# Depthwise convolutions as column-tiled products over shifted copies, state sums in fours, and a different placing of third stages in a four-layer kernel on one core

## The chip, the cores and the metric

The kernel runs on one core of one Trainium2 chip. A core has four compute engines with queues of their own: TensorE (PE; its weight loads are listed as PEld), VectorE (DVE), ScalarE (ACT) and GpSimd (POOL). SyncE (SP) computes nothing; here it issues nearly all DMAs, which sixteen DMA engines carry out. The metric is device time in microseconds for one execution of the whole program; lower is better.

## The reference, cut to what matters

The input `x` is 4 images of 96 channels, 64 x 64 pixels, float32. Four layers follow each other, each on the group-normalised `x` and added to it:

```python
x = x + _L0_conv_ref(_gn(x), ...)
x = x + _L1_conv_ref(_gn(x), ...)
x = x + _L2_conv_ref(_gn(x), ...)
x = x + _L3_conv_ref(_gn(x), ...)
```

Layer 0 is attention with queries pooled 2 x 2 (3 heads of 32 channels, 1,024 queries, 4,096 keys), a softmax over nine neighbours, and a depthwise 5 x 5 convolution of the values:

```python
lepe = lax.conv_general_dilated(v, lepe_w, (1, 1), [(2, 2), (2, 2)], feature_group_count=C)
...
out = feature + lepe
out = jnp.einsum('oc,bchw->bohw', proj_w, out) + proj_b[None, :, None, None]
```

Layer 1 is a selective scan of 192 channels with 16 states each, in four directions over the 4,096 pixels, between convolutions:

```python
xi, z = jnp.split(jnp.einsum('bchw,oc->bohw', x, in_proj_w), 2, axis=1)
xi = jax.nn.silu(conv2d(xi, conv_w, conv_b, groups=E, pad=1))
xs = jnp.stack([xf, xf[..., ::-1], xt, xt[..., ::-1]], axis=1)
...
y = jnp.einsum('bkdln,bknl->bkdl', h, c) + Ds[None, :, :, None]
...
t = jax.nn.relu(bn(conv2d(u, c1_w, c1_b), ...))
t = jax.nn.relu(bn(conv2d(t, c2_w, c2_b, groups=2 * E, pad=1), ...))
t = conv2d(t, c3_w, c3_b)
s = t.mean((2, 3))
...
return t + t * s[:, :, None, None]
```

`c1` takes 192 to 384 channels with a 1 x 1 kernel, `c2` is a depthwise 3 x 3 of 384 channels, `c3` takes them to 96. Layer 2 is one 3 x 3 convolution (sharpening). Layer 3 begins with two 1 x 1 products, goes through two depthwise 3 x 3 convolutions of the same 96 channels, one to a gated branch (`dw2`, `ag1`, `ag2`) and one to a second selective scan with a depthwise 3 x 3 of its own, and ends with a layer norm and the block `crm`. So four places hold depthwise convolutions: `lepe` (5 x 5, 96 channels), the one in front of each scan (3 x 3, 192 channels), `c2` (3 x 3, 384) and `dw1`, `dw2` (3 x 3, 96 each).

## The kernel before, in words

**The scan units.** The function `streams` runs eight scans in the order of `SCANS`: layer 1 of images 0 and 1, layer 3 of images 0 and 1, then the same for images 2 and 3. A scan is four directions x four chunks of 1,024 pixels x two halves of 96 channels, that is 32 groups; a group is twelve units, a unit 8 channels x 16 states on 128 partitions over 1,024 pixels. That makes 384 units a scan and 3,072 in all. One call of `unit(i)` issues, in this order:

- `fetch(i + 4)` (L1938 to L1940): a DMA of 512 KB on SP that copies 8 channels' step sizes from DRAM to all 128 partitions of a tile `rep` (10 buffers);
- DMA issues that were postponed with `later(n, f)` and have become due (`catch_up`), and the store of a finished `yo`;
- `decays(i + 2)` (L1948): exp in place on `rep`, ScalarE;
- `scan(i)` (L1969): the recurrence along the pixels, VectorE, into `hs`; `carry_on` copies its last column, ScalarE;
- `times_c(i)` (L1981): `hs` times C, GpSimd, back into `rep`;
- `collect(j)`, in every third unit, four units late: the sums over 16 states on TensorE. Three units' products stand beside each other in three groups of 32 columns and write three blocks of 32 partitions of the accumulator `acc`;
- `drive(i + 2)`: two small products that spread step size times input over the states, TensorE, into `bx` in PSUM;
- `times_b(i + 1)` (L1962): `bx` times B, VectorE;
- at the end of a group `output`: `acc` goes to `yo` and with it to DRAM (`y_row`, `y_col`, 96 rows).

`prepare` makes what a group of units needs (step sizes, their bf16 parts, B and C) a group or two ahead. In the region of the units the order of instructions on every engine is the order of this program (`tc.manual_schedule`); nothing reorders it.

**The other work beside the units.** All other layers are written as generators that yield after short steps: `first(b)` (layer 0, then the projection and the convolution in front of the first scan), `second(b)` (what follows the first scan up to what the second needs: layer norm, `c1`, `c2`, `c3`, squeeze, sharpening, `dw1`, `dw2`), `third(b)` (what follows the second scan) and `last(b)`. A generator yields nothing when it has issued a product whose result another engine then takes, a number of slots when it has done so, or a tuple when it has just issued one of a chain of products. `BESIDE` says what runs beside which scan; a scan's budget grows by `PACE` slots in each unit (3.5 beside a `first`, 3.7 beside a `second`, 3.2 beside the thirds), less 2.1 in the units that collect. What has not been used up 19 units before the end of a scan is issued there at once (`work.run()`). `first(0)` runs before all units, the rest of `last(3)` after them.

```python
BESIDE = ((("first", 1),), (("second", 0),), (("second", 1),), (("first", 2),),
          (("first", 3),), (("second", 2),), (("second", 3),), (("third", 0), ("third", 1), ("third", 2), ("last", 3)))
```

**Depthwise convolutions before.** The image stands in a tile with a border (`vpad`, `upad`, `hp`, or the two `band` tiles that hold ten rows each). `diagonals` (L1112) makes, on GpSimd, a table of diagonal 96 x 96 matrices, one a tap. `conv` issues one product a tap over a shifted window of the tile, all into one bank of PSUM: 25 for `lepe`, 9 elsewhere, each one slot. Every product goes through the helper `mm` (L948), so all of TensorE's work has that line; it is told apart by the names of its tiles. Before the units begin (`solo`), VectorE takes 11 of the 25 taps or 4 of the 9. `second` has 384 channels as four groups of 96, so 32 convolutions of 9 products an image, then `dw2` with its gates, then `dw1`, then `in_conv` (projection of all rows, then the convolution of all).

Of the kernel before, what the change touches and what calls it, by code (L numbers as in the profile page):

```python
# [26 lines left out]
BIG = LEPE + L  # L27
CH = 1024
# [10 lines left out]
          (("first", 3),), (("second", 2),), (("second", 3),), (("third", 0), ("third", 1), ("third", 2), ("last", 3)))  # L39
# [13 lines left out]
def _weights(i):  # L53
# [13 lines left out]

    p = {}
# [9 lines left out]
    def scan(tag, in_w, conv_w, conv_b, xp, dtw, dtb, alog, d):  # L78
        p[tag + "in"] = in_w.T
        p[tag + "conv"] = halves(conv_w.reshape(E, 9))  # L80
        p[tag + "conv_b"] = halves(conv_b)

# [34 lines left out]
    for n in ("dw1_w", "dw2_w"):  # L117
        p["l3_" + n] = a[n].reshape(C, 9)
    p["l3_ag1"] = a["ag1_w"].reshape(C // 2, C).T
# [24 lines left out]
def _constants(i):  # L144
# [28 lines left out]

    for tag, w in (("l1_", i["L1_conv_A_log"]), ("l3_", i["L3_conv_ss_Alog"])):
        c[tag + "alogn"] = w.reshape(4, E // 8, 8, N).transpose(3, 2, 0, 1).reshape(128, 4, E // 8)
# [4 lines left out]
    c["spread"] = s.reshape(128, 128)  # L180
    return c
# [712 lines left out]
def streams(ctx: ExitStack, tc: tile.TileContext, x, wts, cst, out, wat, cat, flag):  # L894
# [13 lines left out]
    n0, n1, n2 = (cat[k][0] for k in ("ones", "addn", "l1_alogn"))  # L908
# [40 lines left out]

    solo = [True]  # L950
# [37 lines left out]
    def batch_norm(tag, bias):  # L988
        s, b = derived(4), derived(4)
        inv_std(s, wv(tag + "v"))  # L990
        nc.vector.tensor_mul(s, s, wv(tag + "g"))
        nc.vector.tensor_sub(b, bias, wv(tag + "m"))
        nc.vector.tensor_mul(b, b, s)
        nc.vector.tensor_add(b, b, wv(tag + "b"))
        return s, b

    bn1 = batch_norm("l1_bn1_", wv("l1_c1_b"))
    bn2 = batch_norm("l1_bn2_", wv("l1_c2_b"))
# [8 lines left out]
    with tc.tile_pool(name="start", bufs=1) as T:  # L1007
        t0 = T.tile([128, cst.shape[1] - n2], F32, name="t0")
        nc.scalar.dma_start(out=t0, in_=cst[:, n2:])
# [7 lines left out]
        for tag in ("l1_", "l3_"):  # L1017
# [7 lines left out]
            dsum[tag] = derived(2)  # L1025
            nc.vector.tensor_reduce(dsum[tag], wv(tag + "d"), AX.X, ALU.add)


    def image(name):
        return [dram.tile([96, L], F32, name=f"{name}{b}") for b in range(B)]  # L1030

    res1, res2, gate1, skip3, gate3 = (image(k) for k in ("res1_", "res2_", "gate1_", "skip3_", "gate3_"))
    u_row, u_col, y_row, y_col = ([image(f"{k}{h}_") for h in range(2)] for k in ("urow", "ucol", "yrow", "ycol"))
# [73 lines left out]
    def diagonals(pool, w, name="diag"):  # L1107

        taps = w.shape[1]
        w = w[:, :taps]  # L1110
        d = pool.tile([96, taps, 96], F32, tag=name, name=name, bufs=1)
        nc.gpsimd.tensor_tensor(  # L1112
            d,
            ident[:96, :96].unsqueeze(1).to_broadcast([96, taps, 96]),
# [238 lines left out]
    def first(b):  # L1353

        with tc.tile_pool(name="p1", bufs=1) as P:
# [4 lines left out]
            with tc.tile_pool(name="p1d", bufs=1) as D:  # L1360
                samp = D.tile([96, 34, 34], F32, name="samp")
                dist = D.tile([96, 34, 34], F32, name="dist")
                for t in (samp, dist):
                    border(t, 1)
# [836 lines left out]
```

## Time and profile before

Three runs of the kernel before took 14,713.78 to 14,727.14 us, median 14,725.35 us. The profile is of one execution, whose span is 14,698.9 us.

| quantity | value |
|---|---|
| span of the profiled execution | 14,698.9 us |
| median of three runs | 14,725.35 us |
| `scan` with carry, L1969, VectorE | 2,304 x 2,344 ns |
| `times_c`, L1981, GpSimd | 3,072 x 2,357 ns |
| `times_b`, L1962, VectorE | 3,072 x 1,212 ns |
| `decays`, L1948, ScalarE | 3,072 x 1,143 ns |
| `drive`, products into `bx`, TensorE | 6,144 records, 1,412.7 us |
| state sums, products into `acc`, TensorE | 12,288 records, 2,586.7 us |
| depthwise products, `band`, `upad`, `hp`, `vpad` | 2,304, 2,016, 1,152, 1,200 records; 3,291.1 us |
| `rep` fetches | 3,072 x 512 KB |

A group of instructions in the profile has its line, engine, operation, tiles written and read with their shapes, the number of instructions, their busy time, the mean of one in ns, and the idle time of the engine just before them with what ended most of it. A float32 product leaves two records for each call of `mm`. The clock shown for TensorE is what the chip granted it, as a share of full speed; a stretch of the run is given by its start and end in us, and its row has the length, the busy time of PE, PEld, DVE, ACT and POOL with the number of instructions, the granted clock, the DMA engines' busy share and GB/s.

### The profile page before, as it was taken

Reading aid. Unit: us, or ns where it says so; the run is one execution under the profiler, and the core shown is the slowest. Engines: PE = TensorE matmul, PEld = TensorE weight load, DVE = VectorE, ACT = ScalarE, POOL = GpSimd, SP = SyncE. Lnnn points to the kernel's source line nnn. Section 1 sums busy time; section 2 is a strip of 40 time slices with the busy share of each in tenths; the row PEclk is TensorE's granted clock in tenths of the full one; section 3 lists DMA queues with packets and bytes.
Section 4 is the critical chain, followed back from the end, with each engine's and each line's share of the span. In section 5 each row is a group of like instructions: output and inputs, shape, how many; then the busy total and the mean of one; then the engine's idle time right before and its main releaser. Section 6 shows DMA issues by size and latency. Waiting matters only on the chain.

```text
span 14698.9 us, 128101 instructions
## 1 busy us (share of the span) xinstructions
PE 12296.5 (84%) x40802; PEld 3348.5 (23%) x40802; DVE 11654.4 (79%) x7509; ACT 8721.7 (59%) x12340; POOL 10204.0 (69%) x4634
## 2 busy tenths in 40 slices
PE   8888987988889796889868887897979888777767
PEld 2322221222223121222212222222212222111111
DVE  0477888888878888778887888788888888778776
ACT  3355565556756666554755556566755567666554
POOL 0166787777868778667776788687777777666564
PEclk9878887988879787778867887897979888677666
DMA  0266787787878778667876778687787878776674
GB/s 9 72 158 163 188 212 198 188 204 184 221 175 200 197 199 209 154 166 193 211 189 160 178 200 220 172 205 189 203 200 189 204 190 215 175 181 169 165 182 108
DMA packets 902735, 2644.27 MB, mean 180 GB/s; under 512 B 107104, under 2 KB 257216, under 8 KB 902048
## 3 DMA queue, kind: packets, MB, share of 16 engines
q1 hardware_dynamic: 901392, 2634.72, 71.8%
q8 instruction: 324, 5.31, 0.2%
q14 instruction: 363, 2.97, 0.1%
q10 hardware_dynamic: 656, 1.27, 0.0%
HBM read 2168.97 MB, written 466.62 MB: 179 GB/s over the span
## 4 chain that ended last, share of the span: by engine, by line
PE 50%; DVE 20%; ACT 10%; DMA 7%; issue 6%; POOL 5%; SPq 1%; DVEq 0%; POOLq 0%; ACTq 0%
PE one L948 33%; DVE hs L1969 14%; PE acc L948 9%; PE bx L948 6%; DVE bx L1962 5%; DMA rep<-dd 3%; PE held L948 3%; POOL rep L1981 2%; ACT rep L1948 2%; ACT L1948 1%; ACT ex L1287 1%; ACT L1890 1%; DMA xz<-gate 0%; ACT delta L1888 0%; POOL delta L1893 0%
## 5 line engine op out<-in xcount | busy, mean ns | idle before, releaser
L1981 POOL TENSOR_TENSOR rep<-hs,bc 128x1024 f32<-128x1024 f32 x3072 | 7224.5, 2357 | 3210.5 <-DVE hs L1969 2664.2
L1969 DVE TENSOR_TENSOR_SCAN hs<-rep,carry,bx 128x1024 f32<-128x1024 f32 x2304 | 5401.7, 2344 | 274.0 <-POOL rep L1981 14.8
L1962 DVE TENSOR_TENSOR bx<-bx,bc 128x1024 f32<-128x1024 f32 x3072 | 3723.6, 1212 | 1086.2 <-PE bx L948 1063.5
L1948 ACT ACTIVATE rep<-rep,l_decay 128x1024 f32<-128x1024 f32 x3072 | 3495.7, 1143 | 513.3 <-DMA rep<-dd 493.8
L948 PE MATMUL bx<-parts,spread 24*128 24x512 bf16 x6144 | 1412.7, 435 | 1662.7 <-DVE hs L1969 1608.8
L948 PE MATMUL acc<-rep,ct 128*32 128x512 f32 x12288 | 2586.7, 741 | 9.8 <-POOL rep L1981 9.1
L1969 DVE TENSOR_TENSOR_SCAN hs<-rep,bx 128x1024 f32<-128x1024 f32 x768 | 1754.7, 2285 | 123.3 <-ACT carry L1977 29.0
L948 PEld LDWEIGHTS <-spread 24*128 24x128 bf16 x6144 | 310.4, 93 | 4154.6 <-DVE hs L1969 2755.2
L948 PE MATMUL one<-band,dg 96*96 96x512 f32 x2304 | 1075.9, 605 | 0.0
L948 PE MATMUL one<-upad,diag 96*96 96x512 f32 x2016 | 996.4, 632 | 0.0
L948 PE MATMUL one<-qq,kk 96*128 96x512 f32 x1152 | 818.8, 800 | 134.6 <-ACT ex L1287 84.0
L948 PEld LDWEIGHTS acc<-rep,ct 128*32 128x32 f32 x12288 | 506.2, 127 | 1742.4 <-issue 1494.2
L1287 ACT ACTIVATE ex<-one 128x512 f32<-128x512 f32 x576 | 343.1, 596 | 747.7 <-PE one L948 743.0
L948 PE MATMUL one<-pr,ct 6*96 6x512 f32 x1024 | 652.7, 728 | 84.3 <-DVE V L1192 10.4
L1948 ACT ACT_TABLE_LOAD x495 | 635.1, 1283 | 76.6 <-DMA rep<-dd 68.5
L948 PE MATMUL one<-hp,diag 96*96 96x512 f32 x1152 | 607.1, 668 | 28.6 <-POOL diag L1112 28.6
L948 PE MATMUL one<-vpad,diag 96*96 96x512 f32 x1200 | 611.7, 647 | 0.0
L1977 ACT COPY carry<-hs 128x1 f32<-128x1 f32 x2304 | 409.2, 178 | 308.4 <-DVE hs L1969 306.5
L948 PE MATMUL held<-ex,cols 128*32 128x256 f32 x3072 | 567.9, 450 | 7.9 <-ACT ex L1287 1.9
L948 PE MATMUL held<-ex,vT 128*32 128x256 f32 x3072 | 568.3, 451 | 0.0
L948 PEld LDWEIGHTS one<-band,dg 96*96 96x96 f32 x2304 | 346.6, 162 | 535.3 <-issue 516.8
L948 PEld LDWEIGHTS one<-upad,diag 96*96 96x96 f32 x2016 | 314.7, 169 | 489.2 <-issue 478.3
(3420 smaller groups left out, 14369.3 us busy)
## 6 DMA issues: line engine op xcount, KB each, us to landing
rep<-dd SPq DMA_DIRECT2D x3072, 512.0 KB
parts<-du SPq DMA_DIRECT2D x1024, 144.0 KB
bc<-rows SPq DMA_DIRECT2D x256, 512.0 KB
dd<-delta SPq DMA_DIRECT2D x256, 384.0 KB
du<-cut SPq DMA_DIRECT2D x256, 384.0 KB
us<-urow SPq DMA_DIRECT2D x128, 384.0 KB
du<-cut SPq DMA_DIRECT2D x256, 192.0 KB
yrow<-yo SPq DMA_DIRECT2D x128, 384.0 KB
```

The source lines that it names most:

```text
L948: nc.tensor.matmul(o, lhsT=lhsT, rhs=rhs, start=first, stop=last)
L1287: nc.scalar.activation(last.rearrange("p a b -> p (a b)"), p, AF.Exp, scale=HD**-0.5)
L1890: nc.scalar.activation(w, w, AF.Ln)
L1948: nc.scalar.activation(a, a, AF.Exp, scale=decay[tag][:, k, NG * h + m : NG * h + m + 1])
L1962: nc.vector.tensor_mul(bx, bx, ready[i // NG][2][:, 0, :])
L1969: nc.vector.tensor_tensor_scan(out=hs, data0=a, data1=bx, initial=carry[:, h, m : m + 1] if c else 0.0, op0=ALU.mult, op1=ALU.add)
L1977: nc.scalar.copy(carry[:, h, m : m + 1], live[i][1][:, CH - 1 : CH])
L1981: nc.gpsimd.tensor_tensor(a, hs, ready[i // NG][2][:, 1, :], ALU.mult)
```

## The change

**Tables.** `diagonals` and `conv` go, and with them VectorE's share of the taps. `blocks` makes, on GpSimd, tables of 32 columns: for each group of 32 channels and each step in y, three (for `lepe` four) 32 x 32 diagonals stacked on the partitions, one for each shift.

**Shifted copies.** A bordered image has a row pitch of 65 (`ROW`; the column of zeros is shared by neighbouring rows), 66 for `lepe`. Before a convolution, `copies` brings it from SBUF to SBUF by DMAs of 32 partitions each into a tile `around` (2 buffers): three copies of a group of 32 channels, shifted by 0, 1 and 2 columns, stand on 96 partitions. So one product with a table of 96 x 32 covers three taps of 32 channels, and the 3 or 4 groups of 32 channels stand beside each other in 32-column tiles (`shifted`). For `lepe` four copies (0 or 1 row, 0 or 1 column) stand on 128 partitions, and nine products with steps of 2 cover a 6 x 6 kernel whose last row and column are zero.

```diff
+    def soon(f):
+
+        done = []
+        if solo[0]:
+            f()
+            return [True]
+        later(1, lambda: done.append(f()))
+        return done
+
+    def arrived(done):
+        while not done:
+            yield WAIT
+
+    def copies(T, S, at, n, of=range(3)):
+
+        for s in range(3):
+            for g, m in enumerate(of):
+                nc.sync.dma_start(out=T[32 * s : 32 * s + 32, g, :n], in_=S[32 * m : 32 * m + 32, at + s : at + s + n])
+
+    def shifted(o, weight, T, groups, row):
+
+        for y in range(3):
+            for g in range(groups):
+                rhs = T[:, g, (row + y) * ROW : (row + y + 8) * ROW].rearrange("p (r c) -> p r c", c=ROW)[:, :, 0:W]
+                mm(o[32 * g : 32 * g + 32], weight[:, g, y, :], rhs, y == 0, y == 2)
+            if y < 2:
+                yield (1,)
+        yield
```

Copies are issued through `soon`: beside the units they go out one unit later on SP, and the generator yields `WAIT` until then. A `fill` has 9 copies of 18 rows (in front of the scans, `dw1` and `dw2`: two blocks of 8 rows), 12 copies of 10 rows (`c2`: one block) or 12 of 12 rows (`lepe`). Each convolution is run one fill later than its fill.

**What follows from the new shapes.** `c1`'s 384 channels stand as 3 groups of 128 partitions, not 4 of 96, so `c1`, `c2`, the batch norms and `c3` have three steps for four. `dw2` and `dw1` use the same copies and run in one loop, the gates' products after both; `x1` moves to an outer pool. `in_conv` projects and convolves in turn instead of one after the other. The keys `kk` of the attention stand in the tile `feat`. `lepe`'s loads of `x` come with the fills, and the projection of the values alternates with the convolution.

```diff
-                    for q in range(4):
-                        p = bank()
-                        yield from conv(p[:96], dg[q], last[:, q], 0)
-                        nc.scalar.activation(t2[:, q, :], p[:96], AF.Relu,
-                                             bias=bn2[1][:, q : q + 1], scale=bn2[0][:, q : q + 1])
-                        yield 1
...
+                def fill(k):
+                    j, q = divmod(k, 3)
+                    T = pool.tile([96, 4, 10 * ROW], F32, name="around", bufs=2)
+                    src = band[j % 2][:, q, :]
+                    there[k] = T, soon(lambda: copies(T, src, 0, 10 * ROW - 1, range(4)))
+
+                def convolve(k):
+                    j, q = divmod(k, 3)
+                    T, done = there.pop(k)
+                    yield from arrived(done)
+                    if q == 0:
+                        t2[j] = pool.tile([128, 3, PCH], F32, name="t2", bufs=1)
+                    p = bank()
+                    yield from shifted(p, dg[:, 4 * q : 4 * q + 4], T, 4, 0)
+                    nc.scalar.activation(t2[j][:, q, :], p, AF.Relu, bias=bn2[1][:, q : q + 1], scale=bn2[0][:, q : q + 1])
+                    yield 1
```

**State sums in fours.** `collect` runs in every fourth unit, five units late, with four groups of 32 columns; 24 of each 32 rows of `acc` hold sums. `rep` has 12 buffers, `yo` is one tile of 128 rows for the whole run, `y_row` and `y_col` have 128 rows, and what reads them takes 24 of each 32 rows with four DMAs (`ungapped`) where there was one.

```diff
-        rep = sp.tile([128, CH], F32, name="rep", bufs=10)
+        rep = sp.tile([128, CH], F32, name="rep", bufs=12)
...
-        hs = [live.pop(i + q)[0] for q in range(3)]
-        w = addn[:, 24 - 8 * (m // 3) : 56 - 8 * (m // 3)]
+        hs = [live.pop(i + q)[0] for q in range(4)]
+        w = addn[:, 24 - 8 * (m // 4) : 56 - 8 * (m // 4)]
         for e in range(2):
-            for q in range(3):
-                mm(live["acc"][bass.ts(q, 32), bass.ts(e, PCH)], w, hs[q][:, bass.ts(e, PCH)], m == 0, m == NG - 3)
+            for q in range(4):
+                mm(live["acc"][bass.ts(q, 32), bass.ts(e, PCH)], w, hs[q][:, bass.ts(e, PCH)], m == 0, m == NG - 4)
...
-        j = i - BEHIND - 2
-        due = j >= 0 and j % 3 == 0
+        j = i - BEHIND - 3
+        due = j >= 0 and j % 4 == 0
```

**Order and pace.** The third stages of images 0 and 1 move from the last scan to the sixth and seventh, behind the second stages of images 2 and 3. The pace is given for each scan.

```diff
-          (("first", 3),), (("second", 2),), (("second", 3),), (("third", 0), ("third", 1), ("third", 2), ("last", 3)))
+          (("first", 3),), (("second", 2), ("third", 0)), (("second", 3), ("third", 1)), (("third", 2), ("last", 3)))
+PACE = (2.25, 2.05, 2.05, 2.25, 2.25, 2.75, 2.75, 3.2)
...
-            owed = min(owed, 0.5) + PACE[BESIDE[s][0][0]] - (2.1 if i % 3 == 1 else 0.0)
+            owed = min(owed, 0.5) + PACE[s] - (2.1 if i % 4 == 1 else 0.0)
```

The program is also built with a setting of 1,024 for its dynamic DMA scratch.

## The prediction

> **What bounds the kernel now.** I read the shares and slices of the page first, then busy time by stretches, then the products of two tiles at one clock, then the waits.
>
> ```profile
> PE 12296.5 (84%) x40802; PEld 3348.5 (23%) x40802; DVE 11654.4 (79%) x7509; ACT 8721.7 (59%) x12340; POOL 10204.0 (69%) x4634
> ...
> PEclk9878887988879787778867887897979888677666
> ...
> q1 hardware_dynamic: 901392, 2634.72, 71.8%
> ```
>
> TensorE is busiest, but at 0.6 to 0.9 of its clock; VectorE is close behind; the one DMA queue moved 2,634.72 MB in 71.8% of 14,698.9 us, 10,554 us or 4.01 us per MB.
>
> The next view splits the run: busy time (and instructions) of each engine, granted clock, DMA share, GB/s.
>
> ```profile
> 0.00:690.00 690.00, 607.35 (x2724) 217.84 (x2724) 180.45 (x284) 211.56 (x352) 32.12 (x43) 0.95 0.10 28
> 690.00:14569.00 13879.00, 11600.58 (x37948) 3108.96 (x37948) 11444.46 (x7184) 8486.50 (x11948) 10167.06 (x4588) 0.81 0.76 189
> 14569.00:14699.00 130.00, 88.61 (x134) 21.68 (x130) 29.48 (x42) 23.68 (x42) 4.82 (x3) 0.63 0.12 34
> ```
>
> From 690 to 14,569 the 3,072 scan units run, 13,879 us, with VectorE (third busy number) at work for 11,444. Its work there does not change, so only its 2,435 us of idle time can shrink. These two groups show why 3,072 × (2.34 + 1.21) = 10,906 of it stays:
>
> ```profile
> L1969 DVE TENSOR_TENSOR_SCAN hs<-rep,carry,bx 128x1024 f32<-128x1024 f32 x2304 | 5401.7, 2344 | 274.0 <-POOL rep L1981 14.8
> L1962 DVE TENSOR_TENSOR bx<-bx,bc 128x1024 f32<-128x1024 f32 x3072 | 3723.6, 1212 | 1086.2 <-PE bx L948 1063.5
> ```
>
> The second names the idle time: 1,063.5 us waiting for the product `bx` of `drive`, which stands in TensorE's queue behind work of the other layers. Where, by kind of that work, one image each (the columns as above):
>
> ```profile
> 804.00:1621.00 817.00, 717.66 (x3305) 197.03 (x3304) 623.10 (x381) 470.94 (x719) 561.63 (x251) 0.79 0.66 163
> 1621.00:2300.00 679.00, 607.22 (x1864) 169.50 (x1864) 600.22 (x363) 434.25 (x599) 551.65 (x245) 0.88 0.82 211
> 2394.00:2665.00 271.00, 221.34 (x566) 53.54 (x567) 201.36 (x147) 141.23 (x208) 164.26 (x78) 0.77 0.67 166
> 2665.00:3049.00 384.00, 382.63 (x1230) 116.14 (x1229) 337.93 (x195) 234.91 (x341) 312.88 (x137) 0.99 0.80 197
> 3152.00:3589.00 437.00, 346.76 (x1008) 91.15 (x1009) 347.14 (x219) 277.45 (x392) 317.94 (x147) 0.79 0.74 184
> 3589.00:3880.00 291.00, 277.24 (x864) 79.88 (x862) 253.14 (x148) 222.59 (x275) 238.63 (x108) 0.94 0.84 215
> 3880.00:3970.00 90.00, 69.91 (x235) 18.45 (x234) 85.49 (x51) 68.14 (x91) 77.22 (x34) 0.85 0.93 245
> 3970.00:4064.00 94.00, 47.92 (x160) 8.37 (x160) 84.61 (x50) 47.83 (x52) 77.13 (x35) 0.57 0.86 207
> 12531.00:13533.00 1002.00, 784.51 (x2009) 176.17 (x2010) 787.21 (x557) 622.02 (x878) 632.39 (x293) 0.72 0.70 173
> ```
>
> VectorE's idle time is length less busy time. Attention and neighbours (first row): 194 us, three images, 582. Convolutions of `first` (second row) 79, three images, 236; of `second` (rows four, six and seven) 46 + 38 + 5 = 89, four images, 354; together 590. Hand-offs of `second` (rows three and five: layer norm, sharpening, gates): 70 + 90 = 160, four images, 638. Thirds of images 0 and 1 (last row): 215. That leaves 410 in the remaining parts. The reader should see that the convolutions, where TensorE is fullest (382.63 of 384), lose little: 12%, beside 10% in the row with no beside-work (3970). The loss per microsecond is largest where products are handed between engines at a clock of 0.7 to 0.8.
>
> **The change, part by part.** Products first. One view each of the same full-clock stretch, by tile: the depthwise product of `band`, then the state sums `acc`.
>
> ```profile
> 2762.00:3049.00 287.00, 158.51 (x341) 51.30 (x342) 18.30 (x28) 0.00 (x0) 1.00 0.81 199
> 2762.00:3049.00 287.00, 47.03 (x288) 9.65 (x288) 3.65 (x3) 3.31 (x3) 1.00 0.81 199
> ```
>
> A product is two records: 158.51 / 170.5 = 0.93 us for one of 96 columns; 288 records are 48 groups of three 32-column products, 47.03 / 48 = 0.98 us a group. So a group of three costs one product. A group of four has no row; I take 0.98, and 1.31 as its upper bound (four thirds). In the stages the edit turns 3 × (200 + 144) + 4 × (288 + 144 + 144) = 3,336 products, 3,102 us at full clock, into 3 × (72 + 48) + 4 × (72 + 48 + 48) = 1,032 groups, 1,011 us. State sums: 2,048 groups become 1,536, 502 us less. About 2,600 of some 9,400 us at full clock (11,600.58 × 0.81) leave TensorE. The Trainium skill, "TensorE: Matmul & The Clock Gate", Measured speedup vs the span model, gives 2.38 times for three column tiles, where this trace has 3 × 0.93 / 0.98 = 2.85; by the page a group is an estimated 1.17 us and 198 us of the saving goes.
>
> What this is worth depends on VectorE's waits, so by section:
>
> *Start* (690 us, no scan to hide behind): 8 × (14 × 0.93 − 9 × 0.98) + 16 × (5 × 0.93 − 3 × 0.98) = 61 us of TensorE go, and VectorE's share of the taps with them; copies that the next product waits for give some back. I take −40, bounds −90 to +40.
>
> *Attention*, −45% of 582 = −262. The slower pace (3.5 to 2.25 slots a unit, minus 2.1 at each collect, now each fourth unit) spreads the 192 score products in program order over units 40 to 197 instead of 34 to 164: 17% fewer per unit. TensorE was busy 88% there at clock 0.79, 567 us at full clock or 3.37 a unit; less 0.65 for sums (two groups in three units), 0.46 for `drive` (its group: 1,412.7 us over 3,072 units) and some 0.3 for the scan's preparation, about 2.0 are work. It falls by 0.33, the sums to 0.49: 2.9, 14% less. If TensorE sets the pace, 817 becomes 703 and 59% of the idle time goes (−343); if exp-to-product latency does, nothing (0). That it is TensorE which is late (88% busy, the waits for `bx`) puts me nearer the first.
>
> *Hand-offs of `second`*, −45% of 638 = −287. The 88 products of directions and layer norm move from units 3–36 to 4–52, 31% fewer per unit; the sharpening from 180–204 to 161–215. Demand per unit is 221.34 × 0.77 / 48 = 3.55 us in the layer norm; a third less of its 2.1 of work brings 5.65 us a unit to about 4.5, where VectorE's own work is 4.2. If demand decides, three quarters go (−480); if each hand-off costs what it costs, nothing (0).
>
> *Convolutions*, 0, from −335 to +674. TensorE stops being full, which would leave 5% idle, as in the row of 3880 (590 − 255 = −335). But the shifted copies are new traffic: 2,256 DMAs of 83 to 150 KB, 242 MB, and 48 MB for `y` in 128 rows. At 4.01 us per MB that is 1,163 us more, 11,717 in all. The scan alone needs 163 GB/s × 817 us / 168 units = 0.79 MB a unit at share 0.66, 3.2 us. The 24 MB for `band` now fall on some 84 units: + 0.285 MB, 1.14 us, 4.4 a unit, where the units run at 4.0 today. Packed to the share of 0.93 that the row of 3880 bears, it is 4.75; done so for every section (copies and own traffic: 177 units of each `second`, 117 of each `first`) it is +674. If copies inside SBUF go faster than these loads from DRAM, the gain stands. No row shows such a copy, so I take today's pace. On VectorE nothing is added; GpSimd's tap tables get smaller. The Trainium skill, "DMA: Bandwidth & Descriptors", Measured, speaks against the copies: 138 GB/s at 64 KB, 341 at 1 MB, and the advice to batch to a megabyte. Nothing here shows a lone copy's rate; at 138 GB/s the 242 MB would be an estimated 1,754 us instead of 972.
>
> *Moving two thirds*, −60, from −250 to +150. The 1,002 us of 192 units in the last stage become units with no beside-work, 94 / 24 = 3.92 each, 752: −250. They carry 106 us of VectorE work (787 − 192 × 3.55) and most of their 215 us idle time into the sixth and seventh scan, where pace 2.75 replaces 3.2; that gives most of it back.
>
> *SP's queue.* Copies are issued one unit after they are asked for, behind waits for ScalarE's rows and for the products that free `around`; behind them stand the `rep` fetches (512 KB, four units ahead), for which ScalarE's exp waits. Cover: `rep` has 12 buffers for 10. Taken as 0 beyond the bounds above; uncovered it is the slow rival. The wider `yo` and the split loads of `y` add issues only.
>
> Sum: −40 − 262 − 287 + 0 − 60 = −649; 14,698.9 − 649 = 14,050. The median of the runs is 26 us above the profiled span, so 14,076.
>
> **Rivals.** *VectorE's floor*: waits fall everywhere to 7.5% (between the rows of 3880, 5%, and 3970, 10%): 11,444 / 0.925 + 650 + 130 + 26 = 13,180. For it: TensorE loses over a quarter of its work. Against it: idle is largest where there were no convolutions.
> *Transfers bind in the convolutions*, +674 in place of 0: 14,750. For it: share 0.93 is all any long stretch shows. Against it: share 1 for some units is possible with 12 buffers.
> *Slower: fetches starve behind copies.* Place: SP, at each of the 192 fills in the stages (16 in each `first`, 36 in each `second`). A fill of 12 copies of 83 KB is 1 MB, 4.0 us of the engines ahead of the next `rep`. Exp already waits for `rep` 243 times, 494 us, 10.1 at the longest. From 649 / 192 = 3.4 us of VectorE stall a fill the gain is gone; at 5.5 it is 1,056 lost: 15,130. Against it: four units ahead are 14 us.
> *It doesn't do what it says*: column groups run one after another. Then a unit's 1.5 slots are 4.5 products, 4.2 us, beside 1.4 of the scan: 5.6 for today's 4.05, over 1,059 units + 1,640, 15,700. The `acc` row all but excludes it.
>
> **How the numbers follow.** Forecast 0.64; floor 0.15; transfers 0.07; starving 0.12; serial groups 0.02. Faster takes the first two and a little of the third: 0.80; the third straddles the line of 0.2%, which is about what a measurement of this kernel can tell from no change: same 0.05; slower 0.15. The forecast's own range is 13,600 to 14,500; to hold 8 in 10 it reaches down to the floor and up into transfers: 13,200 to 14,700.
>
> **What would show it.** Right: `around` products in groups of about 1 us at full clock, VectorE busy some 11,400 us, its wait for `bx` well under 1,063 us, DMA share above 0.8, exp's wait for `rep` under 1,000. Wrong: ScalarE or VectorE waiting on `rep` in units 60 to 144 of `second` (starving); DMA share at 0.93 with convolution units at 4.7 us (transfers); attention still at 4.9 us a unit (latency, not load).

## The result, and the profile after

The changed kernel is slower: 15,658.17 us median (15,656.29 to 15,674.75, four runs) beside 14,719.57 us for the kernel before on the same chip (four runs); ratio 1.0648, 95% interval 1.0633 to 1.0663. The profiled execution's span is 15,654.5 us, 955.6 above that of before. Taken from the starts of the scans, the eight scans changed by +82, +157, +145, +64, +71, +381, +366 and -307 us; start and tail by -0.4 and -3.6. So every scan that has convolutions beside it is slower, the sixth and seventh most, and only the last, which lost two third stages, is faster.

The shares, the clock and the queue, from the page of the changed kernel:

```profile
PE 11153.2 (71%) x41042; PEld 2767.3 (18%) x41042; DVE 11545.6 (74%) x7341; ACT 8667.4 (55%) x12267; POOL 10152.0 (65%) x4587
...
PEclk9776676776666665766667676776767667666556
...
q1 hardware_dynamic: 1029264, 2927.68, 75.2%
```

The same kind of stretches as before (length, busy time and instructions of PE, PEld, DVE, ACT and POOL, granted clock, DMA share, GB/s): start, scan region, tail; then attention beside the first scan (units 24 to 192), the first 48 units of the second scan (layer norm), its units 48 to 144 (`c2`), units 48 to 96 of the sixth scan (`c2` at the faster pace), and units 96 to 312 of the last, with nothing beside the scan:

```profile
0.00:689.90 689.90, 574.38 (x3060) 204.41 (x3060) 70.04 (x116) 211.34 (x352) 28.36 (x42) 0.91 0.23 58
689.90:15528.60 14838.70, 10491.65 (x37850) 2541.53 (x37850) 11446.49 (x7184) 8432.69 (x11875) 10118.78 (x4542) 0.67 0.78 195
15528.60:15654.50 125.90, 87.22 (x133) 21.34 (x132) 29.05 (x42) 23.36 (x40) 4.86 (x3) 0.64 0.12 36
796.87:1614.90 818.03, 718.20 (x2987) 172.43 (x2986) 614.10 (x372) 448.96 (x672) 549.48 (x239) 0.69 0.68 166
2475.74:2753.45 277.71, 194.92 (x484) 42.49 (x484) 194.86 (x138) 138.23 (x201) 158.01 (x69) 0.65 0.68 168
2753.45:3271.97 518.52, 343.20 (x1378) 100.98 (x1376) 347.48 (x215) 244.20 (x359) 316.30 (x141) 0.71 0.84 199
9980.37:10305.17 324.80, 222.15 (x960) 74.57 (x960) 169.74 (x97) 134.79 (x195) 156.09 (x69) 0.78 0.76 181
14336.39:15148.14 811.75, 398.99 (x1440) 76.76 (x1440) 763.52 (x449) 442.00 (x615) 704.01 (x317) 0.58 0.90 224
```

VectorE's work is what it was (11,446 us for 11,444). TensorE's is 10,491.65 x 0.67 = 7,029 us at full clock where it was 9,396: the work did go. But the `c2` units take 518.52 / 96 = 5.4 us, and 324.80 / 48 = 6.8 in the sixth scan, where they took 4.0, and they are not full on any engine: TensorE is busy two thirds of the time, VectorE two thirds and half. Attention takes 818 us for 168 units, as before (817). The units with nothing beside them run at 3.76.

The groups, in the form of those shown of before (busy time, mean ns; then idle time before them and what ended most of it):

```profile
L2138 DVE TENSOR_TENSOR_SCAN hs<-rep,carry,bx 128x1024 f32<-128x1024 f32 x2304 | 5401.9, 2345 | 495.5 <-ACT carry L2146 186.7
L2131 DVE TENSOR_TENSOR bx<-bx,bc 128x1024 f32<-128x1024 f32 x3072 | 3723.1, 1212 | 1691.3 <-PE bx L978 1665.1
L2117 ACT ACTIVATE rep<-rep,l_decay 128x1024 f32<-128x1024 f32 x3072 | 3498.5, 1143 | 1274.7 <-DMA rep<-dd 1255.7
L978 PE MATMUL one<-around,taps 96*32 96x512 f32 (+1 forms) x6768 | 1497.8, 805 | 499.1 <-DMA around<-band 317.1
```

VectorE waits 1,665 us for `bx` where it waited 1,063. The third row is new in size: exp waited 494 us for `rep`, now 1,256. And TensorE's new products wait for their copies.

One stretch of the `c2` units of the second scan shows how. First SyncE's queue, where each row is a run of DMA issues (start, us from the first to the end of the last, line, tiles, how many):

```profile
2917.81 0.80 SPq L2090 DMA_DIRECT2D parts<-du  x2
2918.65 0.60 SPq L2026 DMA_DIRECT2D rows<-pr  x2
2919.58 11.60 SPq L1188 DMA_DIRECT2D around<-band  x12
2931.28 1.20 SPq L2109 DMA_DIRECT2D rep<-dd  x2
2932.58 1.19 SPq L2031 DMA_DIRECT2D bc<-rows  x2
2933.86 0.55 SPq L2109 DMA_DIRECT2D rep<-dd  x1
2934.50 13.48 SPq L1188 DMA_DIRECT2D around<-band  x12
2948.08 1.85 SPq L2109 DMA_DIRECT2D rep<-dd  x3
```

Two fills of twelve copies hold the queue for 11.60 and 13.48 us, and between them only three `rep` fetches get out. Over all 96 fills of `c2` the median is 10.1 us. The median issue takes 588 ns, 7.1 us for twelve; the rest is time between the copies, most of which the trace puts down to earlier DMAs that had yet to land. `rep` fetches alone come to this much over the run (total us, times, longest):

```profile
SPq L1188 <- DMA rep<-dd: 387.6, 233, 3.8
```

Then ScalarE, VectorE and TensorE in the same stretch (in brackets the idle time before, and what ended it):

```profile
2922.34 1.15 ACT L2117 ACTIVATE rep<-rep,l_decay 128x1024 f32<-128x1024 f32 x1 [1.61 <-DMA rep<-dd]
...
2935.98 1.15 ACT L2117 ACTIVATE rep<-rep,l_decay 128x1024 f32<-128x1024 f32 x1 [11.82 <-DMA rep<-dd]
...
2949.99 0.35 ACT L1671 COPY band<-band 128x192 f32<-128x192 f32 x1 [11.16 <-DMA around<-band]
2950.30 1.15 ACT L2117 ACTIVATE rep<-rep,l_decay 128x1024 f32<-128x1024 f32 x1
```

```profile
2925.72 2.35 DVE L2138 TENSOR_TENSOR_SCAN hs<-rep,carry,bx 128x1024 f32<-128x1024 f32 x1
2937.21 1.23 DVE L2131 TENSOR_TENSOR bx<-bx,bc 128x1024 f32<-128x1024 f32 x1 [9.14 <-PE bx L978]
2938.57 2.35 DVE L2138 TENSOR_TENSOR_SCAN hs<-rep,carry,bx 128x1024 f32<-128x1024 f32 x1
2940.84 1.21 DVE L2131 TENSOR_TENSOR bx<-bx,bc 128x1024 f32<-128x1024 f32 x1
2951.53 2.35 DVE L2138 TENSOR_TENSOR_SCAN hs<-rep,carry,bx 128x1024 f32<-128x1024 f32 x1 [9.49 <-ACT rep L2117]
```

```profile
2930.86 5.98 PE L978 MATMUL one<-around,taps 96*32 96x512 f32 x24 [6.55 <-DMA around<-band]
2936.78 0.39 PE L978 MATMUL bx<-parts,spread 24*128 24x512 bf16 x2
```

The reader sees three waits with one origin. Exp waits 11.82 us for a `rep` whose fetch stood behind the first fill. `drive`'s product stands in TensorE's queue behind products that wait for copies, and VectorE waits 9.14 us for it. And ScalarE waits 11.16 us until the second fill has been read out of `band`, before it may overwrite a border row there; exp and the next scan stand behind that.

### The profile page after: what moved, and what is told of

Its sections match the earlier page's. It is cut to its first block, busy times and chain, and to the rows that moved or that the text cites. A ratio compares the mean times of both kernels' runs of the same rounds, so it can differ in the third digit from the quotient of the medians.

```text
span 15654.5 us, 131884 instructions
## 1 busy us (share of the span) xinstructions
PE 11153.2 (71%) x41042; PEld 2767.3 (18%) x41042; DVE 11545.6 (74%) x7341; ACT 8667.4 (55%) x12267; POOL 10152.0 (65%) x4587
## 4 chain that ended last, share of the span: by engine, by line
PE 31%; DMA 21%; DVE 19%; ACT 10%; issue 7%; POOL 5%; SPq 4%; DVEq 0%; POOLq 0%; ACTq 0%
PE one L978 19%; DVE hs L2138 13%; DMA rep<-dd 10%; PE acc L978 6%; DVE bx L2131 5%; PE bx L978 3%; POOL rep L2150 3%; PE held L978 3%; ACT rep L2117 2%; SPq L1188 2%; DMA around<-hp 1%; DMA rows<-pr 1%; DMA du<-cut 1%; ACT L2117 1%; DMA parts<-du 1%
## 5 line engine op out<-in xcount | busy, mean ns | idle before, releaser
L978 PE MATMUL bx<-parts,spread 24*128 24x512 bf16 x6144 | 1606.8, 491 | 2956.8 <-DVE hs L2138 2689.2
L978 PE MATMUL acc<-rep,ct 128*32 128x512 f32 x12288 | 2451.8, 893 | 5.1 <-POOL rep L2150 5.1
L978 PE MATMUL one<-around,taps 96*32 96x512 f32 (+1 forms) x6768 | 1497.8, 805 | 499.1 <-DMA around<-band 317.1
L978 PE MATMUL one<-qq,feat 96*128 96x512 f32 x1152 | 936.7, 906 | 116.0 <-ACT ex L1378 72.5
L978 PE MATMUL one<-pr,ct 6*96 6x512 f32 x1024 | 865.2, 960 | 79.2 <-ACT pr L2022 26.6
L978 PE MATMUL held<-ex,cols 128*32 128x256 f32 x3072 | 628.5, 494 | 6.9 <-ACT ex L1378 1.0
L978 PEld LDWEIGHTS one<-around,taps 96*32 96x32 f32 (+1 forms) x6768 | 366.4, 132 | 1261.1 <-issue 973.3
L978 PE MATMUL one<-us,wt 96*38 96x512 f32 x1024 | 336.2, 783 | 121.2 <-DMA us<-ucol 68.1
L978 PE MATMUL one<-pad,l_k 96*96 96x512 f32 x576 | 369.4, 777 | 0.0
L2177 DVE TENSOR_TENSOR yo<-yo,acc 128x1024 f32<-128x1024 f32 x128 | 155.5, 1215 | 282.3 <-PE acc L978 282.3
```

What stands on the lines that cost most here:

```text
L978: nc.tensor.matmul(o, lhsT=lhsT, rhs=rhs, start=first, stop=last)
L2177: nc.vector.tensor_add(yo, yo, ya)
```

## The experiments: what the copies cost

Each is the changed kernel with one edit. **Without the copies**, the products reading the bordered image itself:

```diff
-                nc.sync.dma_start(out=T[32 * s : 32 * s + 32, g, :n], in_=S[32 * m : 32 * m + 32, at + s : at + s + n])
...
-                rhs = T[:, g, (row + y) * ROW : (row + y + 8) * ROW]...
+                rhs = T[:96, (row + y) * ROW : (row + y + 8) * ROW]...
```

> Leaves out all 2,256 shifted copies; the 32-column products read the bordered image itself, so the convolutions' values are wrong, while the number, shape and order of the products, the sums in fours, the moved thirds and the paces stay as in the change. Theory A (the copies come late, and TensorE, ScalarE and the rep fetches wait behind them): the units of the convolution stretches go from 5.0 to 7.2 us back to about 4, over some 120 units in each of four second stages (about 1.5 us each, 720) and some 50 in each of three first stages (0.5 us each, 75): 15,658 - 795 = 14,860, between 14,600 and 15,000. Theory B (fewer products leave TensorE at a granted clock of 0.68 in place of 0.81, and everything handed over by TensorE is late for that): the clock falls further and the time stays above 15,400. Theory C (the moved thirds and the changed paces cost it): above 15,400 too, with the second and third of the eight scans no faster than now (1,828 us).

14,765.06 us, ratio 1.0046 (1.0029 to 1.0064). The copies cost 893 us, nearly all that was lost. Three of the stretches above in this run (attention, units 24 to 192; `c2`, units 48 to 144 of the second scan; `c2`, units 48 to 96 of the sixth):

```profile
746.69:1563.89 817.20, 716.18 (x2983) 170.54 (x2981) 614.18 (x372) 448.66 (x672) 548.82 (x239) 0.69 0.67 167
2650.99:3046.32 395.33, 304.37 (x1378) 75.15 (x1376) 345.74 (x215) 242.58 (x359) 316.04 (x141) 0.79 0.82 201
9392.24:9584.31 192.07, 173.05 (x974) 48.74 (x966) 167.36 (x97) 133.50 (x194) 157.35 (x70) 0.94 0.79 193
```

The `c2` units are back at 4.1 and 4.0 us, and the second and third scan take 1,640 and 1,638 us where they took 1,828 and 1,829: theory A holds, theory C falls. But the clock over the whole run is 0.696, little above the 0.684 of the change, at a time 893 us shorter: so the low clock is not what made the change slow, and theory B falls as its cause. The same run shows the rest of the failure: with no copies at all the kernel is no faster than before.

**The same copies, which nobody reads:**

> The same copies as in the change, of the same bytes at the same places, but the products read the bordered image itself and so never wait for a copy (the convolutions' values are wrong). Theory A in its first form (TensorE, in order, waits for the copies: 450 us of such waits in the trace of the change): most of the loss goes, below 15,050. Theory A in its second form (12 issues at a time hold up SyncE's queue, so that the rep fetches come late and exp waits 1,256 us for them): stays above 15,400, with exp's wait for rep still above 1,000 us. Theories B and C: no change, above 15,400.

15,554.29 us (1.0583, 1.0565 to 1.0600). Taking away TensorE's wait for the copies is worth 104 us only, though ScalarE's wait until they have left `band` grew from 161 us to 357 at the same time. The waits of ScalarE in this run (total us, times, longest):

```profile
ACT rep L2117 <- DMA rep<-dd: 1393.9, 514, 24.1
...
ACT band L1671 <- DMA around<-band: 356.9, 28, 18.9
```

The copies do harm by being there: 789 us over the run without them. Theory A's first form falls, the second stands. **The same bytes in a third of the DMAs**, and **half the bytes in as many DMAs**, both on the run with unread copies:

```diff
-        for s in range(3):
-            for g, m in enumerate(of):
-                nc.sync.dma_start(out=T[32 * s : 32 * s + 32, g, :n], in_=S[32 * m : 32 * m + 32, at + s : at + s + n])
+        for g, m in enumerate(of):
+            nc.sync.dma_start(out=T[:96, g, :n], in_=S[:96, at + g % 3 : at + g % 3 + n])
```

> As the run with unread copies (15,554 us), but each fill moves the same bytes with a third of the DMAs (96 partitions each instead of 32); still nothing reads them, and the convolutions' values are wrong. The copies cost 789 us there over the run without copies (14,765). Theory A1 (the number of issues: 12 of 0.6 us in a row on SyncE, with only some of them in flight, hold up the rep fetches): two thirds of the 789 go, 15,030, below 15,150. Theory A2 (the bytes: 242 MB more through the 16 DMA engines): no change, 15,500 to 15,600.

```diff
+        n = n // 2
         for s in range(3):
```

> As the run with unread copies (15,554 us), with the same number of DMAs, each of half the length; the convolutions' values are wrong. Theory A1 (issues): no change, 15,450 to 15,600. Theory A2 (bytes): half of 789 goes, 15,160, below 15,250.

15,234.46 us (1.0357, 1.0340 to 1.0375) and 15,376.63 us (1.0451, 1.0434 to 1.0469): 320 us for two thirds of the issues, 178 us for half of the bytes. Neither expectation is met alone; both causes are real. As an estimate, in proportion, all of the issues would be 480 us and all of the bytes 355, together 835 where 789 were to be explained. No run shows that either goes in proportion, and since an issue can wait for earlier bytes to land, the two are not separate. Exp's wait for `rep` falls with the issues, from 1,394 to 1,172 us.

**Issued by GpSimd** instead of SyncE (`nc.gpsimd.dma_start` in both places):

> The change with its copies issued by GpSimd instead of SyncE: the same number, bytes and readers. If SyncE's queue is what the issues hold up (rep fetches behind a fill): some 300 us or more go, 15,350 or less, and exp's wait for rep falls below 1,000 us. If the DMA engines' own handling of the many copies is it: no gain, 15,600 or above; and since a copy that waits for its data now holds up the products with C on GpSimd, it may be slower still, up to 16,000.

16,042.76 us (1.0904, 1.0885 to 1.0922), slower still, while exp's wait for `rep` falls from 1,256 to 914 us. The gain expected of a free SyncE did not come: SyncE was relieved, and the wait went elsewhere. GpSimd, in order too, now waits for earlier copies, its issues take it 0.50 us each, TensorE waits longer for the copies, and the scan waits 381 us for GpSimd where it waited 33:

```profile
L978 PE MATMUL one<-around,taps 96*32 96x512 f32 (+1 forms) x6768 | 1487.2, 790 | 700.1 <-DMA around<-band 471.0
...
L1188 POOL DMA_DIRECT2D around<-band x1152 | 568.7, 500 | 309.0 <-DMA around<-band 279.0
...
DVE hs L2138 <- POOL rep L2150: 381.4, 119, 10.0
```

The Trainium skill, "DMA: Bandwidth & Descriptors", Rules for kernel authors, says that spreading DMAs over the issuing engines gains no bandwidth and only saves sequencer issue time; the 342 us less of waiting for `rep` fit such a saving, and the total shows that more was paid on the other queue. So this run does not isolate what SyncE's queue costs.

**Three band tiles**, so that ScalarE need not wait for the copies (`band` with three tiles, the border row written into the next one; 11 `rep` buffers to make room):

> The change with three band tiles instead of two (and 11 rep buffers instead of 12 to make room), so that ScalarE's copy of the border row and its writes into the next band no longer wait until the copies out of the band have landed. Where ScalarE waits, exp and the carry queue behind it. Theory A3 (this wait of ScalarE passes the lateness of the copies on to the scan: 161 us at the border copy, 246 us more of scan waiting for the carry than before): 200 to 400 us go, 15,250 to 15,450. If the copies only hurt through SyncE and TensorE: 15,600 or above.

15,689.36 us (1.0669, 1.0651 to 1.0687). No gain. The ScalarE wait of the timeline is real, but it is a wait beside others; theory A3, 200 to 400 us, falls. The buffer that was given up can hide a small gain: with sums in fours alone, below, two buffers were worth 104 us.

## The experiments: what was left without copies

**A third of the depthwise products**, on the kernel before:

```diff
-            mm(o, lhsT, rhs, t == 0, t == len(taps) - 1)
+            if solo[0] or every:
+                mm(o, lhsT, rhs, t == 0, t == len(taps) - 1)
+            elif t % 3 == 0:
+                mm(o, lhsT, rhs, t == 0, t + 3 >= len(taps))
```

> The kernel before with only every third product of the depthwise convolutions beside the scans (their values are wrong; image 0's, before the scans, and the sharpening are whole), each left-out product still taking its slot, so that the order of everything else is kept and no copy is made. Some 2,224 of 3,336 products, 2,070 us at full clock, leave TensorE. The prediction's floor (TensorE's load is what makes VectorE wait): 590 us of idle time in the convolution stretches fall to 255, 14,370 or less. If less load only means a lower clock, or VectorE waits there for something else: 14,600 to 14,750.

14,442.33 us (0.9827, 0.9810 to 0.9843): 265 us less, for some 2,224 products. The work on TensorE was worth taking away, at 0.12 us a product; the forecast's bound for the convolutions was 335. The granted clock fell to 0.742 in this run, and it was the faster one: a lower clock and a shorter time went together.

**The paces of the change** on top of it (2.25 and 2.05, raised by 0.175 because threes collect more often; left-out products take no slot):

> The run with every third depthwise product (14,442 us), with the left-out products taking no slot and with the paces of the change (2.25 and 2.05, raised by 0.175 for sums in threes): the same work spread over as many units as in the change, without copies, fours or moved thirds. The prediction's steps for attention and hand-offs (fewer products a unit, less idle time a unit): up to 549 us less, 13,900 to 14,200. If each step of attention and layer norm costs the scan a fixed stall whatever stands beside it: 14,380 to 14,500.

14,669.88 us (0.9976, 0.9963 to 0.9988): 228 us *more* than with the old paces, where up to 549 less had been forecast. The paces hardly spread attention here (its score products lie in units 35 to 169, before in 33 to 164; in the change in 39 to 197). In the second stages work moved to later units, where it met the scan again: beside the second scan units 0 to 48 took 255 us for 275 and units 144 to 264 took 487 for 527, but units 48 to 144 took 390 for 371 and units 264 to 384 took 530 for 463.

**Sums in fours alone**, on the kernel before, with the 12 `rep` buffers, the y in 128 rows and the small DMA scratch that go with them, paces lowered by 0.175:

```diff
-            for q in range(3):
-                mm(live["acc"][bass.ts(q, 32), bass.ts(e, PCH)], w, hs[q][:, bass.ts(e, PCH)], m == 0, m == NG - 3)
+            for q in range(4):
+                mm(live["acc"][bass.ts(q, 32), bass.ts(e, PCH)], w, hs[q][:, bass.ts(e, PCH)], m == 0, m == NG - 4)
```

> The kernel before with the state sums in fours alone (with 12 rep buffers, y in 128 rows, the smaller DMA scratch, and paces lowered by 0.175 so that the mean budget of a unit is what it was). The prediction's step: 502 us of TensorE work at full clock go, which was to be worth about a fifth of the 549 us forecast for attention and hand-offs, some 100 to 250 us: 14,470 to 14,620. Theory B (less TensorE work means less clock and so no gain): 14,720 or above.

14,991.54 us (1.0200, 1.0181 to 1.0219): 288 us slower, the opposite sign. Of that, 134 us lie in the three scans with attention, 82 in the last scan. Attention (units 24 to 168) and `c2` (units 48 to 144 of the second scan), first before, then with fours:

```profile
804.27:1504.76 700.49, 620.96 (x2934) 159.35 (x2934) 528.91 (x322) 405.98 (x627) 469.85 (x204) 0.80 0.66 162
2664.85:3049.48 384.63, 383.26 (x1232) 116.25 (x1230) 338.43 (x196) 235.06 (x341) 313.51 (x137) 0.99 0.80 197
```

```profile
805.18:1550.33 745.15, 658.15 (x3029) 172.39 (x3029) 531.98 (x321) 410.68 (x642) 473.38 (x209) 0.75 0.64 156
2742.60:3118.30 375.70, 367.12 (x1218) 111.95 (x1216) 337.15 (x196) 235.73 (x342) 313.26 (x137) 0.99 0.84 205
```

Where TensorE is full and at full clock, fours gain 9 us in 96 units. In attention they lose 45 in 144 (part of it because the score products come a little sooner, in units 31 to 156 where they lay in 33 to 164), and the clock falls. Is the clock the cause? **Zero-weight products put the work back:**

```diff
+        if j >= 0 and j % NG in (2, 6):
+            for q in range(4):
+                mm(live["acc"][bass.ts(q, 32), :PCH], nil, ready[i // NG][2][:, 0, :PCH], False, False)
```

> The run with sums in fours alone (14,992 us), with two groups of four products with zero weights added to acc for every 12 units (in units without a collect), so that TensorE has as much to do for the sums as with threes. It adds 512 groups, some 500 us at full clock. Theory B (the clock: with less work TensorE is granted full clock for less of the time, 0.787 against 0.81, and its other products get slower): the time falls, to 14,750 to 14,900, though TensorE does more. If the loss of fours lies elsewhere (the loads of y in four parts, later sums, other slots): no gain, 14,990 or above, up to 15,200.

15,312.57 us (1.0416, 1.0398 to 1.0433), 321 us more again, though the clock rose from 0.787 to 0.795. More work on TensorE costs time, 0.63 us a group, and what the clock regained did not make up for it. That was only 0.008 of the 0.030 lost, so the clock as a part of the 288 is not ruled out. The Trainium skill, "TensorE: Matmul & The Clock Gate", The HAM clock gate, says that idle windows of about 3.4 us throttle the clock to half; the granted clock here does fall as TensorE empties (0.817, 0.787, 0.684 over the whole run), but the run that kept it busier got slower.

Five runs looked for the rest of the 288. The DMA scratch alone, on the kernel before:

> The kernel before with nothing changed but the setting of its dynamic DMA scratch to 1,024. The run with sums in fours alone, which had it too, lost 288 us. If the setting is what costs there (fewer DMAs in flight, say): 14,850 to 15,000. If it does nothing: 14,690 to 14,740.

14,703.32 us (1.0000, 0.9991 to 1.0010): nothing. Fours with ten `rep` buffers and the old scratch:

> The sums in fours alone, with 10 rep buffers and the DMA scratch as before (which the room in SBUF just allows), y in 128 rows and loads in four parts as in the change. If fours themselves cost 288 us (their later sums, their slots, the loads of y): 14,950 to 15,100, a little above 14,992 for the two buffers fewer. If the scratch cost it: 14,500 to 14,750.

15,095.52 us (1.0262, 1.0243 to 1.0280): fours themselves. Loads of y in four parts, on the kernel before:

> The kernel before (sums in threes, 96 rows) with every load of y, and of u into yo, as four DMAs of 24 partitions instead of one of 96. The run with fours alone lost 15 to 24 us in the first 24 units of each second stage and in the thirds. If the four-part loads cost that: 14,800 to 14,900. If they cost nothing: 14,690 to 14,740.

14,781.09 us (1.0051, 1.0034 to 1.0067): a little under what was expected for it, 74 us. y in 128 rows, on the kernel before:

> The kernel before with y kept in 128 rows (sums in threes, one DMA a load, 32 rows of nothing in each store and in each load into yo): 48 MB more, nothing else. At the 4.01 us of all DMA engines per MB 193 us of transfers. If these bytes are part of what fours lose: 14,780 to 14,900. If they are hidden: 14,690 to 14,740.

14,685.14 us (0.9990, 0.9980 to 0.9999): the bytes are hidden. Fours with an even budget:

> The run with sums in fours alone (14,992 us) with the same mean budget given evenly: 2.8, 3.0 and 2.5 slots in each unit, and none taken off in the units that collect. If fours lose because three units in four then take up to 3.8 slots of other work where two in three did, and a unit with two steps of attention or layer norm in it is the one that stalls: 14,700 to 14,900. If not: 14,950 or above; above 15,050 if the slots taken off at a collect are worth what they are meant to be.

15,056.32 us (1.0231, 1.0214 to 1.0248): the unequal slots are not it. So, if the 74 simply add, 214 of the 288 us stay unexplained, and what in the order of fours costs them is open.

**The third stages back in the last scan:**

> The change with the third stages of images 0 and 1 back in the last scan, as before, and paces 2.05 in the sixth and seventh scan as in the second and third. Theory A: the sixth and seventh scan become like the second and third (1,828 us in place of 2,051 and 2,048), the last like that of before (2,039 in place of 1,732): 15,658 - 223 - 220 + 307 = 15,520, that is the move cost some 135 us. Theory C (the move is what costs): below 15,000.

15,607.18 us (1.0617, 1.0600 to 1.0635): the move, with the paces of 2.75 that came with it (2.05 here), costs 51 us, less than the 135 expected.

## Why the prediction was wrong

The losses and gains add up along one chain of runs: 14,707 (before), minus 265 with a third of the depthwise products (14,442), plus 228 for the paces (14,670), plus 95 for fours and moved thirds (14,765), plus 893 for the copies (15,658). The 95 were not taken apart: the sums in fours, the moved thirds (51, measured with copies), the new shapes of `c1` to `c3` and the merged loops lie in them, and a start that is 50 us shorter. How much of the 288 of fours is left at the new paces is not known. Units 24 to 192 beside attention, 47 us longer with fours alone, are back at 817.20 in the run without copies; but with the thirds back the last scan, set to 3.2 as before, takes 76 us longer than before, where fours alone had cost it 82.

- *Products* (2,600 us to go; a group of three at 0.98): right. 2,367 us went; the new products' 1,497.8 us make 1,032 groups (288 of them of four products) of 1.45 us at a clock of 0.67, 0.97 at full clock. The 2,447.64 us of sums in the scan region are 1,535 groups of 1.59, 1.07 at full clock, near the 0.98 taken and under the bound of 1.31.
- *SP's queue* (0, "uncovered it is the slow rival"): this is the step that failed first. The cover was priced as transfer time: 1 MB, 4.0 us of the DMA engines ahead of the next fetch, against 14 us of lead. What counted was the queue: 11.60 and 13.48 us for one fill, two fills with three fetches between them. Of the 893 us some 50 fall into the start; the other 843 are 4.4 us for each of the 192 fills, past the 3.4 from which the rival was to decide and under its 5.5. The rival's place was right and its price near; the queue had been set to 0 in the sum. Its time, 15,130, is short by 528, though its price a fill was too high, because it still counted 649 of gains that did not come.
- *Attention* (-262, from -343 to 0) and *hand-offs* (-287, from -480 to 0): wrong; the lower end of each, "if exp-to-product latency does, nothing", was the nearer. In attention TensorE did the work that was forecast to remain: 718.20 x 0.69 = 496 us at full clock for 567, 12.5% less where 14% had been computed. But 168 units took 818 us as before, and 817.20 without copies, and TensorE's busy time did not move at all (717.66 and 718.20). The 88% that argued for load was read at a clock that falls with the load. That exp-to-product latency sets the pace there instead is not shown. Over the three images these units gained 25 us of the 262 forecast (818, 815 and 810 us for 817, 834 and 817); with fours at the old paces the first took 864. In the hand-offs of images 0 and 1 the layer norm's 48 units took 277.71 us for 271. The gates' and sharpening's units 144 to 264 took 50 us less, but units 264 to 384, to which part of that work had moved, took 66 more; the second scan, before and after:

```profile
3049.48:3589.13 539.65, 430.06 (x1282) 115.36 (x1281) 438.30 (x281) 340.45 (x488) 397.06 (x182) 0.81 0.76 191
3589.13:4064.80 475.67, 395.14 (x1258) 106.56 (x1256) 423.91 (x247) 339.34 (x418) 393.78 (x176) 0.85 0.86 219
```

```profile
3271.97:3761.90 489.93, 341.61 (x1098) 76.19 (x1098) 431.16 (x265) 301.36 (x434) 393.33 (x180) 0.68 0.86 212
3761.90:4303.53 541.63, 347.84 (x1329) 71.47 (x1326) 428.84 (x253) 361.68 (x445) 391.44 (x173) 0.64 0.88 223
```

- *Convolutions* (0, from -335 to +674): the gain was 265, and by the estimate above the bytes cost some 355, so these two alone come near the 0; the issues, an estimated 480, were not in it. The rates that the prediction quotes from the Trainium skill, "DMA: Bandwidth & Descriptors", Measured, are for loads from HBM issued by GpSimd. Of copies inside SBUF the runs show 178 us of end time for half of 242 MB, some 1.5 us a MB.
- *Start* (-40): 0. Without copies it is 50 us shorter (640.4 us up to the first scan), so the copies give back all of it, as the bounds allowed.
- *Moving two thirds* (-60, from -250 to +150): 51, within the bounds, on the other side.
- Of the signs named in advance, groups of about 1 us and VectorE's 11,400 us came true; the DMA share, 0.78, stayed under the 0.8 named; the wait for `bx` went the wrong way, and exp's wait for `rep` passed the 1,000 us that were to tell of starving. Two signs of being wrong came true: ScalarE waited for `rep` in the convolution units of `second`, and attention stayed at 818 / 168 = 4.9 us a unit.

## A version that is faster than both

If late fetches hold up exp in the kernel before too, more lead should help. **Twelve buffers** alone, then **thirteen and a fetch five units ahead**, both on the kernel before with the small DMA scratch to make room:

```diff
-        rep = sp.tile([128, CH], F32, name="rep", bufs=10)
+        rep = sp.tile([128, CH], F32, name="rep", bufs=13)
...
-    AHEAD, BEHIND, LEAD = 4, 2, 6
+    AHEAD, BEHIND, LEAD = 5, 2, 6
```

> The kernel before with 12 rep buffers in place of 10, in the room that a DMA scratch of 1,024 frees, and nothing else: the one part of the change that gives SyncE more freedom. With sums in fours 12 buffers were 104 us faster than 10 (14,992 against 15,096). If they are worth as much with threes, fetches no longer wait for the sums (3,376 us of such waits on SyncE before) and this is faster than both kernels: 14,600 to 14,680. If exp's 494 us of waiting for rep is covered anyway: 14,690 to 14,730.

> As the run before it with 13 rep buffers and every fetch issued five units ahead instead of four. If a rep that comes late is what holds up exp: 14,550 to 14,650, and exp's wait for rep well under 494 us. If it only moves the fetches into the way of other transfers: 14,690 or above.

14,695.65 us (0.9994, 0.9985 to 1.0003): buffers alone do nothing. With the fetch a unit earlier 14,631.15 us (0.9949, 0.9935 to 0.9962), 70 us less than before. Exp's wait for `rep` before and in this run:

```profile
ACT rep L1948 <- DMA rep<-dd: 493.8, 243, 10.1
...
ACT rep L1948 <- DMA rep<-dd: 90.0, 64, 6.8
```

Four hundred microseconds of that wait are gone and 70 of time: most of it was covered. The changed kernel itself was not run with the longer lead, nor with `rep` fetches let in between the copies of a fill; whether either would save it is open.

## What to carry to other kernels

Price a transfer that is split up by its issues on the queue it shares as well as by its bytes: a copy here cost 893 / 2,256 = 0.40 us of end time, and a product that it made unnecessary was worth 0.12, so copies that each replace about one product, as here, cannot pay. A prefetch behind bursts in a queue that works in order may need a longer lead, or an issue order that lets it past; here a unit more of lead gained 70 us in the kernel before, and neither was tried beside the copies. And a busy share read at a clock that moves with load is no proof that load sets the pace: take the load away in the kernel before, without what replaces it, before pricing it.

## What the runs showed of the hardware that was not expected

Twelve copies of 81 KB in a row took SyncE 11.60 and 13.48 us to issue, where the median of one is 588 ns, 7.1 us for twelve; most of the rest is, by the trace, waiting for earlier DMAs of the queue to land. The same bytes in a third as many DMAs made the program 320 us faster with nothing reading them. TensorE's busy time in attention stayed at 718 us when its work at full clock fell by an eighth, the granted clock going from 0.79 to 0.69. And sums in four column groups, some 520 us less work at full clock (2,582.99 x 0.81 before, 2,015.70 x 0.78 with fours alone), made the kernel before 288 us slower, of which 214 were not found.
